# A graph layer on one core: two PSUM banks for the gathers, the marks in shared banks, narrower unread products, and a new order of all steps

## The chip, the cores and the metric

The kernel runs on one NeuronCore of a Trainium2 chip. The metric is the device time of one launch in microseconds (us). Three runs of the kernel before took 502.46, 503.40 and 503.78 us, the median is 503.40. One further execution was profiled and took 503.59 us.

The engines are named as in the profile: PE is TensorE (PEld is its loading of weights, which overlaps its products), DVE is VectorE, ACT is ScalarE, POOL is GpSimd, SP is SyncE, which issues the DMAs. L946 is line 946 of the kernel before.

## The reference, cut to what matters

128 graphs have 64 nodes each, a node has 128 channels, and about one in eight of the node pairs is an edge. Every edge sends a message through an MLP with two layer norms, messages are summed by receiving node, and a second MLP of the same form updates the node.

```python
def _mlp(x, w0, b0, g0, be0, w1, b1, g1, be1, w2, b2):
    h = relu(x @ w0 + b0)
    h = layernorm(h, g0, be0)
    h = relu(h @ w1 + b1)
    h = layernorm(h, g1, be1)
    return h @ w2 + b2

# x: (128, 64, 128), adj: (128, 64, 64) of 0 and 1
f_i, f_j = x[:, :, None, :], x[:, None, :, :]          # broadcast over the pairs
messages = _mlp(concat(f_i, f_j), *msg) * adj[..., None]
agg = sum(messages, axis=2)
return x + _mlp(concat(x, agg), *upd)
```

## The kernel before, in words

**Units of work.** Only edges are computed, not all 64 x 64 pairs. Each graph has 640 slots for its edges. Two graphs make a pair (64 pairs, index p), four pairs make a block (16 blocks, b), 512 slots make a chunk (160 chunks, n, ten to a block), and five chunks make a group (32 groups, q), for which the small statistics are worked out together.

**The edge path of one pair and its chunks.**
- `rank` (L744, DVE) and `count` (L753, PE) number the edges. `distance` (L889, ACT) and `make_tp` (L895, DVE) write for each slot the row i of its edge as a 0/1 table (tile tp).
- `marks` (L920, PE): for each half k of a pair's slots, one product of 128x320 in float16 gives the position of every slot within its row. Its result lies in PSUM in a tile mk. `compare` (L928, DVE) reads it and writes the 0/1 table for j. A bank of marks is free when the compare is done.
- `node_rows` (L904, POOL) and `stack` (L911, SP) put both tables below each other into one tile S of the pair by DMA (s<-i and s<-j). `node_marks` (L1034, SP) turns a table with a DMA transpose (oh).
- `rows` (L847, PE) computes x @ w0 for the nodes of half a block, split afterwards into a high and a low part (abh, abl; `rows_hi` L866 and L869, `rows_lo` L876, L877, L880).
- `gather` (L946, PE): product of abl and abh with S, which is the first layer of the edges of a chunk, in the bank hps. `relu0` (L951, ACT) reads it and writes h.
- `turn_h` (L956, PE) turns h into hT for `stats0` (L613, DVE). `seed` (L989 POOL, L993 ACT) prepares the bias, scaled by the standard deviation of the first norm.
- `layer1` (L1003, PE) is the second layer, in the banks z0 and z1; `relu1` (L597 DVE or L1012 ACT) writes y, `stats1` (L613, DVE) its statistics.
- `weights` (L1045, POOL) scales the receiving table by the second norm, and `reduce` (L1060, PE) sums the messages of a block into the bank ys.

**The node update of a block.** `turn` (L1109, PE) and `turn_out` (L1114, ACT) turn an operand of the update MLP (first ysum, then uh, then uy); `layer` (L1123, PE) applies a layer; `finish` (L1173, DVE) writes the result uo, and a DMA stores it. `turn_x` (L832, PE) turns the nodes' x.

**PSUM.** There are eight banks, one tile each, given out by pools (L663 to L669): `ps_k` for mk, `ps_h` for hps, `ps_t` for hT, two `ps_z`, `ps_y` for ys, `ps_a` (tile ma, by `abank`) and `ps_u` (tile mu, by `ubank`). ma takes the update turns, count, turn_x and the first half of the rows; mu takes the update layers and the second half of the rows. A step that asks for a bank waits until the last reader of the tile before it is done.

**The order.** Each step is entered with `at(n, place, fn)`: a slot n, about one per chunk, and a named place within the slot. A table `MOVE` (L24 to L357, 921 entries) shifts single steps to another slot, place or rank. The steps are then run in this order, and each one appends its instructions to the queues of the engines that it uses. So the order on PE, DVE, ACT, POOL and SP is fixed in the program, and an engine waits at the head of its queue until the semaphores of that instruction have come.

On PE, a block in the steady part runs in this order (T turn_h, L layer1, G gather, M mark): reduce, rows, rows, M, G, T, L, G, turn of ysum, T, L, G, L, T, M, G, update layer of xn and ysum, T, turn of uy, L, G, T, L, M, G, update layer, T, count, M, G, L, L, T, turn of uh, M, G, L, T, M, G, update layer, L, M, T, turn_x, L, G, T, M.

**Unread products.** `keep_busy` (L1322) puts products on PE that nobody reads, into the bank ys. A call with k over 4 makes k products of 128 columns, any other makes k // 2 products of 256 columns. Calls with numbers 7, 2, 4, 2, 4, 4 and 2 are entered before the first slot, and some more in the first slots; MOVE puts some of them much later.

Of the kernel before, what the change touches and what calls it, by code (L numbers as in the profile page):

```python
# [9 lines left out]
F32 = mybir.dt.float32  # L10
# [6 lines left out]
PSUM = bass.MemoryType.PSUM  # L17
# [7 lines left out]
    "<lambda>@@1": (1, "s", 1), "<lambda>@@10": (-1, "m", -1), "<lambda>@@11": (0, "T", 2),  # L25
    "<lambda>@@2": (1, "x", 2), "<lambda>@@3": (1, "S1", -1), "<lambda>@@4": (1, "k", 2),
    "<lambda>@@5": (0, "k", 2), "<lambda>@@6": (-1, "S1", -1), "<lambda>@@7": (-1, "T", 2),
    "<lambda>@@8": (0, "k", -5), "<lambda>@@9": (152, "L0", 3), "ahead@@0": (2, "x", 7),
    "ahead@@1": (2, "x1", -1), "ahead@@2": (1, "x1", 0), "ahead@@3": (2, "L1", -1),
    "ahead@@4": (1, "k", 3), "ahead@@6": (0, "T", 2), "bias0.@3": (-7, "a", 2),  # L30
    "bias0.@@143": (-1, "e0", 4), "bias0.@@153": (-9, "a", 2), "bias0.@@158": (-6, "e", -1),
    "bias0._0@@163": (-1, "T", 2), "bias0._2@@164": (-4, "L0", -1), "bounds@@152": (-136, "b", -1),
    "compare.0@0": (0, "e0", 0), "compare.0@2": (2, "k", 0), "compare.0@5": (1, "T", 0),
    "compare.0@7": (0, "m", 0), "compare.0@@0": (2, "x", 6), "compare.0@@10": (2, "e0", 3),
    "compare.0@@12": (2, "s", 1), "compare.0@@140": (-2, "S1", -1),
    "compare.0@@142": (-2, "k", -1), "compare.0@@145": (-3, "T", 0),
    "compare.0@@147": (-2, "x2", 2), "compare.0@@150": (2, "s", -1),
    "compare.0@@152": (2, "m", -2), "compare.0@@2": (2, "b", 2), "compare.0@@5": (1, "S1", 1),
    "compare.0@@7": (1, "L0", 0), "compare.1@1": (2, "T", -3), "compare.1@3": (3, "y", 2),
    "compare.1@6": (0, "x2", 2), "compare.1@8": (1, "s", 1), "compare.1@@1": (2, "x", 5),  # L40
    "compare.1@@11": (2, "T", -3), "compare.1@@13": (3, "a", 4), "compare.1@@138": (-1, "S1", 1),
    "compare.1@@141": (-2, "T", -1), "compare.1@@143": (-1, "b", 1),
    "compare.1@@146": (-1, "x", 2), "compare.1@@148": (3, "x", 2), "compare.1@@151": (2, "e0", 3),
    "compare.1@@153": (3, "b", 4), "compare.1@@3": (2, "x1", -2), "compare.1@@6": (2, "a", -1),
    "compare.1@@8": (2, "S1", 2), "compare_here@@-1#26": (3, "s", 1),
    "compare_here@@-1#31": (3, "s", 1), "compare_here@@-1#41": (3, "k", 4),
    "compare_here@@-1#47": (3, "x", -1), "count@8": (-2, "e0", -3), "count@@-1#6": (0, "e", -9),
    "count@@1": (1, "k", 5), "count@@138": (-2, "S1", -6), "count@@8": (1, "s", -3),
    "count_out@9": (-3, "e0", -1), "count_out@@-1#7": (0, "e", -9),
    "count_out@@139": (-3, "x", -4), "count_out@@2": (0, "x", 0), "count_out@@9": (0, "e1", 3),  # L50
    "degrees@9": (-6, "T", -2), "degrees@@-1#11": (1, "a", -1), "degrees@@139": (-3, "s", -2),
    "degrees@@2": (0, "s", 2), "degrees@@9": (0, "x1", 0), "distance@0": (-4, "k", -3),
    "distance@3": (1, "k", -1), "distance@5": (-3, "x", -2), "distance@8": (-2, "b", 1),
    "distance@@-1#13": (1, "x2", 0), "distance@@-1#27": (1, "e1", 1),
    "distance@@-1#33": (3, "y", 2), "distance@@1": (1, "k", 4), "distance@@10": (-3, "a", 1),
    "distance@@13": (2, "e", 2), "distance@@138": (-2, "a", -1), "distance@@140": (-3, "s", -1),
    "distance@@143": (-5, "S1", -2), "distance@@145": (-2, "y", 3), "distance@@148": (-7, "k", -1),
    "distance@@150": (-1, "x", 2), "distance@@3": (2, "k", 5), "distance@@5": (1, "y", -3),
    "distance@@8": (0, "x1", -1), "finish.@8": (2, "s", -2), "finish.@@138": (0, "x", -2),
    "finish.@@148": (6, "a", -1), "finish.@@158": (3, "S1", -1), "finish.@@168": (-1, "L0", -2),  # L60
    "finish.@@174": (32, "x1", 0), "finish._0@@175": (41, "e", -2), "finish._2@@176": (43, "y", 1),
    "flag_in@@153": (0, "T", -2), "flag_max@@156": (1, "x2", -1), "flag_out@@160": (2, "S1", -1),
    "flag_sum@@158": (4, "T", 0), "flag_turn@@155": (1, "k", 2), "gather@0": (-1, "m", -2),
    "gather@1": (-1, "b", 0), "gather@2": (1, "e", -1), "gather@3": (2, "L0", 4),
    "gather@4": (2, "m", 4), "gather@5": (1, "y", 1), "gather@6": (0, "T", 0),
    "gather@7": (-1, "k", -4), "gather@8": (-2, "x2", -2), "gather@9": (-2, "m", -2),
    "gather@@-1#28": (3, "y", 3), "gather@@-1#35": (3, "x1", -4), "gather@@-1#43": (4, "x", 1),
    "gather@@0": (3, "e0", 4), "gather@@1": (4, "L1", -5), "gather@@10": (1, "x2", -3),
    "gather@@11": (1, "e0", 3), "gather@@12": (2, "L1", -1), "gather@@13": (2, "e", 2),
    "gather@@138": (-2, "x2", -1), "gather@@139": (-3, "e1", -6), "gather@@140": (-3, "x2", 0),  # L70
    "gather@@141": (-3, "x2", -2), "gather@@142": (-2, "s", -1), "gather@@143": (-2, "s", 2),
    "gather@@144": (-2, "L0", -3), "gather@@145": (-3, "T", 0), "gather@@146": (-3, "S1", -2),
    "gather@@147": (-3, "a", 1), "gather@@148": (0, "x2", 0), "gather@@149": (0, "e1", -2),
    "gather@@150": (2, "s", -1), "gather@@151": (2, "m", 4), "gather@@152": (1, "x2", -2),
    "gather@@153": (0, "e1", -2), "gather@@154": (0, "e1", -2), "gather@@155": (1, "s", 1),
    "gather@@156": (0, "T", 0), "gather@@157": (0, "y", -1), "gather@@158": (0, "k", -1),
    "gather@@159": (0, "e", 2), "gather@@5": (0, "x1", -1), "gather@@6": (0, "y", -2),
    "gather@@7": (0, "a", 0), "gather@@8": (0, "k", -6), "gather@@9": (-1, "x1", -1),
    "inverse_of@0": (0, "x1", -1), "inverse_of@5": (1, "k", -2), "inverse_of@@140": (-3, "x", 1),
    "inverse_of@@145": (3, "x2", 1), "inverse_of@@150": (0, "x", -4),  # L80
    "inverse_of@@155": (2, "a", -2), "inverse_of@@160": (1, "L0", 3),
    "inverse_of@@165": (0, "m", 0), "inverse_of@@168": (2, "x2", -1), "keep@@1": (1, "x1", 0),
    "keep@@10": (0, "L0", 1), "keep@@2": (2, "b", -1), "keep@@3": (2, "L1", -6),
    "keep@@4": (1, "L1", -1), "keep@@5": (0, "k", 3), "keep@@6": (-1, "x1", -1),
    "keep@@7": (1, "s", -2), "keep@@9": (-1, "x1", 3), "keep_busy@@-1#0": (21, "x1", 0),
    "keep_busy@@-1#18": (3, "s", 1), "keep_busy@@-1#23": (17, "x2", -2),
    "keep_busy@@-1#30": (1, "e1", 1), "keep_busy@@-1#37": (17, "T", 2),
    "keep_busy@@-1#45": (3, "s", 1), "keep_busy@@-1#9": (17, "k", -5),
    "keep_busy@@2": (-3, "e", -7), "keep_busy@@3": (-4, "e", -3), "keep_busy@@4": (-5, "e", -7),
    "keep_busy@@5": (-4, "m", -1), "layer1@0": (-3, "m", -1), "layer1@1": (-2, "s", 1),  # L90
    "layer1@2": (-2, "e", 0), "layer1@3": (0, "b", -1), "layer1@4": (2, "m", 3),
    "layer1@5": (1, "y", 0), "layer1@6": (0, "L0", -3), "layer1@7": (-1, "k", -4),
    "layer1@8": (-2, "S1", -7), "layer1@9": (-2, "m", -1), "layer1@@10": (-1, "L1", 1),
    "layer1@@11": (1, "k", 0), "layer1@@12": (1, "e0", 0), "layer1@@13": (1, "L0", 3),
    "layer1@@138": (-2, "S1", -3), "layer1@@139": (-3, "x2", 2), "layer1@@140": (-3, "s", -2),
    "layer1@@141": (-4, "e1", 0), "layer1@@142": (-2, "m", 0), "layer1@@143": (-3, "S1", 2),
    "layer1@@144": (-2, "T", -1), "layer1@@145": (-3, "T", 0), "layer1@@146": (-3, "x", 0),
    "layer1@@147": (-3, "a", 1), "layer1@@148": (0, "a", 0), "layer1@@149": (1, "b", -2),
    "layer1@@150": (-1, "e1", -1), "layer1@@151": (1, "k", 2), "layer1@@152": (1, "T", -3),
    "layer1@@153": (1, "x", -2), "layer1@@154": (1, "m", -1), "layer1@@155": (1, "y", 8),  # L100
    "layer1@@157": (0, "y", -4), "layer1@@158": (0, "a", -2), "layer1@@159": (0, "x2", 1),
    "layer1@@160": (0, "x2", -2), "layer1@@161": (0, "L0", 3), "layer1@@162": (0, "T", -5),
    "layer1@@164": (1, "m", 1), "layer1@@165": (0, "b", 2), "layer1@@166": (0, "e0", 1),
# [256 lines left out]
def tile_gnn(  # L360
# [40 lines left out]
    nc = tc.nc  # L401
# [1246 lines left out]
```

## Time and profile before

| what | value |
|---|---|
| median of three runs | 503.40 us |
| lowest, highest | 502.46, 503.78 us |
| profiled execution | 503.59 us |
| its span | 501.7 us |
| mean clock granted to PE | 0.998 of full |
| PE busy | 491.1 us |
| PEld busy | 467.9 us |
| DVE, ACT, POOL busy | 460.5, 397.9, 353.8 us |
| first product on PE | 1.91 us |
| first gather | 11.17 us |
| last reduction, first instruction | 485.30 us |

The span is the time from the first to the last recorded instruction; 1.9 us of the profiled execution lie outside it. An instruction takes longer from its start to its end than from its start to the start of the next one, since products overlap: a turn of four products has 0.60 us from start to end, but the next step begins 0.44 us after it. What a step costs PE is the second number. A product of two 4-byte operands is recorded as two matmul records.

A row of the waits reads: the engine with its tile and line, "<-" the engine whose end released it, then the total in us, how often, and the longest. A row of the timeline begins with the start and the duration in us.

### The profile page before, as it was taken

How to read it: one execution, taken by the hardware profiler on the slowest of the kernel's cores; microseconds unless marked ns; L12 is line 12 of the kernel's file. 1: busy time of each engine (PE TensorE's matmuls, PEld its weight loads, DVE VectorE, ACT ScalarE, POOL GpSimd, SP SyncE). 2: the span in 40 equal slices, each digit the busy share in tenths (PEclk: the TensorE clock that was granted, in tenths of full speed). 3: DMA queues.
4: the chain of work that ended last, by engine and by line, in shares of the span. 5: the costliest groups of instructions: out<-in, count | busy, mean ns of one | idle time of the engine just before them, and what ended most of it. 6: DMA issues, size and time to landing. Idle time of an engine off the chain costs nothing.

```text
span 501.7 us, 15934 instructions
## 1 busy us (share of the span) xinstructions
PE 491.1 (98%) x5969; PEld 467.9 (93%) x5969; DVE 460.5 (92%) x1225; ACT 397.9 (79%) x907; POOL 353.8 (71%) x563
## 2 busy tenths in 40 slices
PE   8899999999999999999999999999999999999995
PEld 5799999999999999999999999999999999999984
DVE  7899789899999999998999999899999989998885
ACT  6999978889787788978778797877879778867753
POOL 3267686877869687786968768696886679674941
PEclk9999999999999999999999999999999999999999
DMA  4668565566948576684857757475564647345201
GB/s 122 157 138 170 122 129 130 114 133 137 164 104 153 126 141 131 130 161 107 160 128 113 157 121 162 104 171 123 121 154 111 156 107 171 88 113 107 63 23 46
DMA packets 91474, 63.55 MB, mean 127 GB/s; under 512 B 57473, under 2 KB 75522, under 8 KB 91394
## 3 DMA queue, kind: packets, MB, share of 16 engines
q1 hardware_dynamic: 91106, 62.36, 58.7%
q8 instruction: 49, 0.80, 0.7%
q14 instruction: 31, 0.25, 0.2%
q10 hardware_dynamic: 288, 0.13, 0.1%
HBM read 7.15 MB, written 4.19 MB: 23 GB/s over the span
## 4 chain that ended last, share of the span: by engine, by line


## 5 line engine op out<-in xcount | busy, mean ns | idle before, releaser
L1003 PE MATMUL z<-w1c,h 128*128 128x128 f32 x1280 | 167.4, 275 | 0.0
L1003 PEld LDWEIGHTS z<-w1c,h 128*128 128x128 f32 x1280 | 158.1, 192 | 4.1
L613 DVE BATCH_NORM_STATS2 st<-hT 128x6 f32<-128x256 f32 x320 | 120.3, 417 | 21.9 <-PE hT L956 18.7
L951 ACT ACTIVATE h<-hps,b0c 128x512 f32<-128x512 f32 x160 | 109.5, 684 | 24.3 <-PE hps L946 23.0
L993 ACT ACTIVATE z<-b1b,m_sd 128x128 f32<-128x128 f32 x320 | 118.8, 371 | 11.6 <-DVE y L597 4.6
L613 DVE BATCH_NORM_STATS2 st<-y 128x6 f32<-128x256 f32 x320 | 117.9, 417 | 0.1
L989 POOL TENSOR_TENSOR u<-b1b,m_sd 128x512 f32<-128x512 f32 x80 | 82.7, 1042 | 29.8 <-ACT m_sd L621 20.2
L956 PE MATMUL hT<-ident,h 128*128 128x128 f32 x640 | 96.6, 273 | 0.7 <-ACT h L951 0.7
L946 PE MATMUL hps<-s,abl 128*128 128x512 f32 (+3 forms) x256 | 93.4, 370 | 1.0 <-DMA s<-j 0.7
L1045 POOL TENSOR_TENSOR w<-oh,m_q 128x192 f32<-128x192 f16 x126 | 62.5, 509 | 39.9 <-issue 27.1
L956 PEld LDWEIGHTS hT<-ident,h 128*128 128x128 f32 x640 | 74.3, 141 | 1.9 <-ACT h L951 1.0
L946 PE MATMUL hps<-s,abh 128*128 128x512 f32 (+3 forms) x256 | 74.4, 322 | 0.0
L1012 ACT ACTIVATE y<-z 128x512 f32<-128x512 f32 x80 | 47.3, 594 | 30.9 <-PE z L1003 30.8
L928 DVE TENSOR_TENSOR j<-mk,cmpt 128x320 fp32r<-128x320 f32 x124 | 58.3, 470 | 1.4 <-PE mk L920 1.2
L597 DVE CUSTOM_DVE_ANT_0 y<-z,u 128x512 f32<-128x512 f32 x80 | 53.9, 674 | 3.9 <-PE z L1003 2.4
L889 ACT ACTIVATE d<-slot,mid 128x640 f16<-128x640 f16 x64 | 52.7, 826 | 0.7 <-DVE mid L799 0.7
L946 PEld LDWEIGHTS hps<-s,abl 128*128 128x128 f32 x256 | 48.7, 190 | 2.9 <-DMA s<-j 0.9
L946 PEld LDWEIGHTS hps<-s,abh 128*128 128x128 f32 x256 | 48.5, 189 | 0.0
L1060 PE MATMUL ys<-y,w 128*32 128x128 f32 x1488 | 44.3, 274 | 0.0
L1060 PEld LDWEIGHTS ys<-y,w 128*32 128x32 f32 x1488 | 39.7, 110 | 3.6 <-POOL w L1045 2.6
L904 POOL CAST i<-tp 128x640 fp32r<-128x640 f16 x58 | 42.4, 745 | 0.0
L920 PE MATMUL mk<-tp,posall 128*128 128x320 f16 x126 | 38.0, 302 | 0.2 <-DVE j L928 0.2
(195 smaller groups left out, 852.2 us busy)
## 6 DMA issues: line engine op xcount, KB each, us to landing
s<-i SPq DMA_DIRECT2D x124, 160.0 KB, 3.0
s<-j SPq DMA_DIRECT2D x124, 160.0 KB, 2.7
xn<-in_x_dram SPq DMA_DIRECT2D x15, 256.0 KB, 3.8
out_dram<-uo SPq DMA_DIRECT2D x15, 256.0 KB, 2.5
an<-in_adj_dram SPq DMA_DIRECT2D x16, 128.0 KB, 2.8
oh<-tp SPq DMA_TRANSPOSE x64, 3.2
xn<-in_x_dram SPq DMA_DIRECT2D x2, 128.0 KB, 2.8
out_dram<-uo SPq DMA_DIRECT2D x2, 128.0 KB, 3.6
```

The lines of the kernel that those rows point to most:

```text
L597: nc.vector._custom_dve(TENSOR_ADD_SAT, out=o, in0=ps, in1=sb, s0=BIG, s1=0.0)
L613: nc.vector.bn_stats(st, src.rearrange("p t c -> p c t"))
L889: nc.scalar.activation(D[p], slot, AF.Abs, bias=blocks[b]["mid"][:, q:q + 1], scale=-1.0)
L928: nc.vector.tensor_tensor(JR[p][:, c], MK.pop((p, k))[:, 0:HC], cmpt[:, c], op=ALU.is_equal)
L946: nc.tensor.matmul(ps[:, c:c + w], lhsT=ab[:, g % 4, :], rhs=s, start=(k == 0), stop=(k == 1))
L951: nc.scalar.activation(H[n], HP.pop(n), AF.Relu, bias=b0c)
L956: nc.tensor.transpose(ps[:, t, :], H[n][:, t * P:(t + 1) * P], ident)
L989: nc.gpsimd.tensor_tensor(U[n], bc(W["b1b"], CH), SR[q][:, k:k + CH].unsqueeze(2).to_broadcast([P, CH, C]), op=ALU.mult)
L993: nc.scalar.activation(z_of(n)[:, t, :], W["b1b"], AF.Copy, scale=SR[q][:, k + t:k + t + 1])
L1003: nc.tensor.matmul(ps[:, t, :], lhsT=h[:, t * P:(t + 1) * P], rhs=W["w1c"], start=added and t == 0, stop=True, skip_group_check=True)
L1045: (nc.vector if p == NP - 2 else nc.gpsimd).tensor_tensor(WT[p][:, g], oh, qs, op=ALU.mult)
L1060: nc.tensor.matmul(YS[b][g * N + m * HN:g * N + (m + 1) * HN, k, :], lhsT=w[:, g, m, u, :], rhs=y, start=(u == 0), stop=(u == TH - 1), til ...
```

## The change

Five things change in the program.
1. The bank of `ps_k` is given up, and `ps_h` has two buffers: the gathers take turns in two banks.
2. `marks` takes the bank ma for a pair's first half (k = 0) and the bank mu for its second (k = 1). Marks thus share ma with the update turns, count, turn_x and the first half of the rows, and mu with the update layers and the second half of the rows.
3. The first part of the last block's reduction, which was put into the bank of `ps_k`, goes into one of the gathers' banks.
4. `keep_busy` makes products of 128 columns only, k of them for k over 4 and k // 2 otherwise.
5. The table MOVE is written anew (923 entries in place of 921; of the 921 keys that both have, one has the same value). This gives a new order on PE, DVE, ACT, POOL and SP.

The number of instructions of each kind stays. On PE, a block of the steady part now runs in this order: reduce, rows, rows, T, turn of an update, L, M (ma), G, L, G, T, turn of an update, update layer, G, G, T, count, M (mu), L, L, T, M (ma), G, L, T, turn of an update, L, T, M (mu), G, M (ma), G, T, M (mu), L, update layer, turn_x, T, L, update layer, G, T, L, M (ma), G, M (mu), G, L, T.

```diff
-        ps_k = es.enter_context(tc.tile_pool(name="ps_k", bufs=1, space=PSUM))
-        ps_h = es.enter_context(tc.tile_pool(name="ps_h", bufs=1, space=PSUM))
+        ps_h = es.enter_context(tc.tile_pool(name="ps_h", bufs=2, space=PSUM))
...
-            MK[p, k] = bank() if bank else ps_k.tile([P, 512], F32, name="mk")
+            MK[p, k] = bank() if bank else ubank() if k else abank()
...
-                YS[b] = ps_k.tile([P, 512], F32, name="mk").rearrange("p (k c) -> p k c", k=PB)
+                YS[b] = hbank().rearrange("p (k c) -> p k c", k=PB)
...
-            if k > 4:
-                for _ in range(k):
-                    nc.tensor.matmul(warm[:, 0, :], lhsT=mean_m, rhs=mean_m, start=True, stop=True)
-            else:
-                for _ in range(k // 2):
-                    nc.tensor.matmul(warm[:, 0:2, :], lhsT=mean_m,
-                                     rhs=first.rearrange("p q j -> p (q j)"), start=True,
-                                     stop=True)
+            for _ in range(k if k > 4 else k // 2):
+                nc.tensor.matmul(warm[:, 0, :], lhsT=mean_m, rhs=mean_m, start=True, stop=True)
```

Of the new table, its `keep_busy` entries as an example of the form (key with its slot: shift in slots, place, rank):

```diff
-    "keep_busy@@-1#0": (21, "x1", 0), "keep_busy@@-1#18": (3, "s", 1), "keep_busy@@-1#23": (17, "x2", -2),
-    "keep_busy@@-1#30": (1, "e1", 1), "keep_busy@@-1#37": (17, "T", 2), "keep_busy@@-1#45": (3, "s", 1), "keep_busy@@-1#9": (17, "k", -5),
-    "keep_busy@@2": (-3, "e", -7), "keep_busy@@3": (-4, "e", -3), "keep_busy@@4": (-5, "e", -7), "keep_busy@@5": (-4, "m", -1),
+    "keep_busy@@-1#0": (13, "S1", 0), "keep_busy@@-1#18": (17, "e0", -1), "keep_busy@@-1#23": (1, "s", -11),
+    "keep_busy@@-1#30": (0, "e", -37), "keep_busy@@-1#37": (17, "b", 1), "keep_busy@@-1#45": (0, "e", -40), "keep_busy@@-1#9": (16, "e", 2),
+    "keep_busy@@2": (-3, "e", -4), "keep_busy@@3": (-4, "e", -5), "keep_busy@@4": (-3, "m", 2), "keep_busy@@5": (-6, "e", -1),
```

## The prediction

> **What bounds the kernel now.** I read the page's busy times first, then the same times by stretches of the span, then the waits of PE, then the timeline of PE.
>
> ```profile
> span 501.7 us, 15934 instructions
> PE 491.1 (98%) x5969; PEld 467.9 (93%) x5969; DVE 460.5 (92%) x1225; ACT 397.9 (79%) x907; POOL 353.8 (71%) x563
> ```
> ```profile
> 0.00:25.00 25.00, 21.46 (x189) 16.47 (x189) 19.98 (x57) 19.18 (x40) 7.09 (x21) 1.00 0.57 139
> 200.00:400.00 200.00, 200.00 (x2533) 193.71 (x2532) 190.67 (x504) 162.94 (x369) 152.12 (x238) 1.00 0.64 136
> 482.00:502.00 20.00, 13.16 (x138) 11.41 (x136) 11.78 (x36) 8.94 (x27) 4.60 (x9) 0.95 0.15 43
> ```
> The columns of the second fence are stretch, length, PE, PEld, DVE, ACT, POOL, clock, DMA share, GB/s. In the middle PE has work at every moment and DVE 95% of the time (190.67 of 200). Only the head and the tail show a PE that waits. The chain of waits is empty on this page, so I checked this with PE's own waits, which are small:
>
> ```profile
> PE ys L1329 <- DVE first L505: 1.9, 1, 1.9
> PE hps L946 <- DMA s<-j: 0.7, 1, 0.7
> PE hT L956 <- ACT h L951: 0.7, 2, 0.5
> ```
> and with the timeline of one block, from one reduction to the next:
>
> ```profile
> 212.21 2.83 PE L1060 MATMUL ys<-y,w 128*32 128x128 f32 x96
> 225.28 0.60 PE L956 MATMUL hT<-ident,h 128*128 128x128 f32 x4
> 225.72 0.60 PE L1109 MATMUL ma<-ident,uy 128*128 128x128 f32 x4
> 226.15 1.06 PE L1003 MATMUL z<-w1c,h 128*128 128x128 f32 x8
> 226.97 0.37 PE L946 MATMUL hps<-s,abl 128*128 128x256 f32 x1
> 228.85 0.30 PE L920 MATMUL mk<-tp,posall 128*128 128x320 f16 x1
> 241.65 2.06 PE L1060 MATMUL ys<-y,w 128*32 128x128 f32 x68
> ```
> A block takes 241.65 - 212.21 = 29.44 us. Start to next start gives what each step costs PE: a turn 0.437 (225.28 to 225.72), a layer1 0.895, a gather 0.476 to 0.53 by its pieces, a mark 0.125, rows 0.93 a half, reduction 2.74. A block holds 10 turns of h, 4 other turns, 10 layer1, 10 gathers, 8 marks, 2 rows, one reduction, one count and update layers of 1.79, 0.895 and 0.895: 6.12 + 8.95 + 4.98 + 1.0 + 1.86 + 2.74 + 0.03 + 3.58 = 29.26. So at most 0.18 us of a block is loss. The whole loss is about 9 us before 25 us, 2.5 us (14 x 0.18) spread over the blocks, about 2.5 us in irregular pieces (25 to 60 us, near 83, and 413 to 455; the largest is 0.5 at 454, ahead of a gather that waits for S), 2.8 us from 482 to 495.6, and 6 us after the last matmul.
>
> **What the Trainium skill says.** "Perfetto Trace Analysis", Identifying the Most-Contended Engine: matmul busy time is a poor measure, weight-load busy time a better one. PEld at 93% over the span, 97% (193.71 of 200) in the middle, agrees that PE is the bound. "PSUM — Partial Sum Buffer", PSUM bank collisions raise a hardware error: two engines may not touch one bank at once, so banks are guarded whole. A mark in a shared bank therefore waits for the whole copy out of it. Before shows such ordering only for other pairs of steps. "TensorE: Matmul & The Clock Gate", Architectural detail: VectorE and ScalarE run their queues strictly in order, so a late compare holds all behind it; the trace fits, the wait on DVE being for PE, 18.7 us for hT. Same page, Part 1: the clock starts at half and rises after a busy window of about 3.4 us. The trace agrees in kind:
>
> ```profile
> 1.91 2.08 PE L1329 MATMUL ys<-first,mean_m 128*128 128x256 f32 x4 [1.91 <-DVE first L505]
> 4.29 2.91 PE L1329 MATMUL ys<-first,mean_m 128*128 128x256 f32 x6
> 9.61 1.56 PE L1329 MATMUL ys<-first,mean_m 128*128 128x256 f32 x6
> ```
> The same record takes 2.08 / 4 = 0.52 us early and 1.56 / 6 = 0.26 us from 9.61 on; two records make one product.
>
> **The change part by part.** All sums are against the profiled run's 503.59 us (span 501.7 and 1.9 outside it). It lies 0.2 above the median of 503.4.
>
> *Unread products.* Products that lie where PE has other work cost their whole length. Before has four of 256 columns (0.435 each, 48.7 to 54.1 us) and seven of 128 (0.224 each, 60.3 to 61.8): 1.74 + 1.57 = 3.31. The built order of after has seven and five of 128 there: 12 x 0.224 = 2.69. That is **-0.62**. The rest lie in the first 10 us, where PE waits anyway: about 2 us less work, nothing gained, but see the second rival.
>
> *Two gather banks.* A gather's bank is free 1.0 us after its last matmul (relu0). Before puts 0.6 us or more of PE work between gathers, and no wait of a gather for relu0 is on the list of waits. At most 0.05 a block is to be had; I take **0**. The cover is the work between gathers; without it a gather would pay 0.4.
>
> *Marks in the banks of turns and update layers.* No instruction is added. In the order of after the closest neighbours in bank ma are an update turn and a mark with 0.895 of PE work between, 1.33 from the turn's start. In the trace the copy (ACT) ends 1.22 to 1.33 after the turn's start, and about 0.05 passes until PE goes on: 0 to 0.05 a block. In mu, a mark and the next layer start 1.02 apart; the compare ends 0.83 after its mark's start if DVE is free, but 1.94 in the median, because it queues on DVE. The same holds for two turns of h 1.70 apart, whose stats need 1.40 plus 0.05. I walked DVE through one block of after by hand (stats pair 0.68, relu 0.60, compare 0.41, finish 1.1): it keeps up, with under 0.1 us to spare where T, M, G, M, G, T, M, L and an update layer follow each other. Behind a late compare stand stats and relus, and for these the next turn and layer1 on PE. The loss lies between 0 (all in time) and 0.5 us a block; below nothing, a block has at most its 0.18 to give. I take 0.05 x 14 = **+0.7**.
>
> *New order, middle.* Of the 2.5 us of irregular loss, some must return, as the same tables load and the same S tiles land. DMA cover, counted as PE work from a pair's second mark to the first gather that reads it, is at least 5.4 us before and 6.2 after in a steady block; s<-i and s<-j take 2.7 to 3.0 us to land and 1.2 to 1.5 to issue, so SP's queue stays off the path. POOL at 71% stays off it too. Bounds -2.5 and +1; I take **-0.8**.
>
> *Head.* The first gather comes after some 0.9 us less of products, but an oh transpose (1.3 us of SP) now goes ahead of s<-j of an early pair. S of pair 2 is issued by 18.2 in both; before waited for it at 21.6. After has 8.5 us of useful work before that gather where before has 9.8. Bounds -0.15 and +1.15; I take **+0.3**.
>
> *Tail.* The last two part reductions (1.4 each) come after the last layer1 instead of around it, but fewer steps stand between them and the turn of ysum, and one POOL step stands ahead of the last finishes: -0.3 +- 1; I take **-0.3**.
>
> Sum: -0.62 + 0 + 0.7 - 0.8 + 0.3 - 0.3 = -0.7, so 502.9 for a run like the profiled one and **502.7** as the median.
>
> **Rivals.** *The shared banks stall on DVE (slower).* The compares at the dense run of marks come late, PE's mark, turn or layer waits, and this repeats in each of 14 blocks. For it: DVE is busy 95%, and one stats pair (0.68) queued ahead of a compare is enough to free its bank 0.6 late. Against: 18.7 us in which DVE waited for hT is reserve. At 0.3 us a block in place of 0.05: 503.4 - 1.4 + 4.2 = 506.2. It decides from about 0.2 us a block (2.9 us, less 1.4).
>
> *The clock rises late (slower).* With products half as long (six in before, about 1.0 each while slow, in 1.9 to 8.3 us; in after 0.5 each) PE is busy some 60% of this stretch, where before it was busy almost wholly from 1.9. If a window then counts as not busy, 3.4 us more run at half speed, once or twice; a part of this stretch is waiting anyway. +1 to +4; at 2.5: 502.7 + 2.5 = 505.2.
>
> *The new order removes the irregular losses (faster).* PE runs at its floor from 25 to 482: -0.62 - 2.5, and a tail shorter by 0.6: 503.4 - 3.7 = 499.7. For it: each loss is one late transfer or table. Against: the head's is bound by the loads.
>
> *Nothing but the products counts.* The banks and the order give what they take: 503.4 - 0.6 = 502.8, not apart from the forecast.
>
> **How the numbers follow.** Forecast (with the last rival) 0.36, stalls on DVE 0.32, late clock 0.12, floor 0.20. About 0.3% (1.5 us) is what a measurement of this kernel can tell from no change: faster is below 501.9, slower above 504.9. The forecast's own range is 501.2 to 504.3, and a quarter of it is faster: 0.10, with 0.19 of the floor case 0.29. Slower: 0.30 of the stalls, 0.08 of the clock, 0.02 of the forecast: 0.40. The rest, 0.31, is the same. The range 499.6 to 507.6 leaves out the lower end of the floor case and stalls beyond 0.4 us a block.
>
> **What would show it.** Right: blocks from reduction to reduction at 29.4 to 29.5, no wait of PE over 0.1 us for a compare or a copy, twelve late products of 0.224. Stalls: blocks at 29.7 or more, waits of PE for j or for copies from ma. Clock: records of 128 columns (0.224 / 2 = 0.112 apart at full clock) still at about twice that after 9 us. Wrong altogether: a gather that waits for S in every block, or a last matmul later against the last layer1.

## The result and the profile after

The changed kernel took 506.69 us in the median of four runs (505.94 to 508.57), the kernel before 503.27 beside it. The ratio is 1.0077, with a 95% interval of 1.006 to 1.0094: 3 to 4.7 us slower. The execution that was profiled took 508.57 us (span 506.8), the slowest of the four. So I had the same kernel profiled once more (507.22 us, span 505.4, median of 12 runs 506.77, ratio 1.0066, interval 1.0049 to 1.0083) and trust only what both traces show.

The page of the changed kernel:

```profile
span 506.8 us, 15927 instructions
PE 491.1 (97%) x5969; PEld 465.7 (92%) x5969; DVE 478.2 (94%) x1225; ACT 399.8 (79%) x907; POOL 354.9 (70%) x563
```

DVE is busy 17.7 us longer than before (460.5), with the same 1225 instructions. The stretches of the same trace (columns as in the prediction; in the second of them the kernel before had PE busy for all 200.00):

```profile
25.00:60.00 35.00, 33.45 (x370) 31.08 (x368) 33.71 (x82) 30.91 (x74) 22.93 (x35) 1.00 0.54 122
200.00:400.00 200.00, 199.95 (x2506) 192.73 (x2509) 198.69 (x504) 162.26 (x364) 152.00 (x237) 1.00 0.62 137
```

PE loses 1.5 us between 25 and 60 us, where before it lost nothing that shows. DVE is at 99% in the middle. Two waits of PE after 20 us that are larger than any of the kernel before there:

```profile
PE hT L958 <- DVE st L616: 1.5, 1, 1.5
PE hps L948 <- DVE u2c L543: 1.1, 1, 1.1
```

Neither is a mark that waits for a copy out of a shared bank, or an update turn or layer that waits for a compare. The second line names DVE, but its u2c was done long before; the gather waited for S (the pair's table, which the gathers read), and the second trace says so (1.7 us, for s<-i).

To see where the time went I took from each trace the start of every step on PE and subtracted the durations of all useful steps before it (471.24 us in both kernels). What is left is the loss: time in which PE waited, ran slowly or ran unread products. The loss in us, by stretches:

| useful work done by PE (us) | before | changed, second trace | changed, with three moves (see below) |
|---|---|---|---|
| 0 to 20 (until about 34 us) | 13.25 | 14.20 | 12.91 |
| 20 to 60 (about 34 to 80 us) | 4.19 | 5.79 | 4.51 |
| 60 to 400 | 3.06 | 4.09 | 2.90 |
| 400 to 460 | 1.42 | 0.98 | 0.97 |
| 460 to the last layer | 2.66 | 3.33 | 3.53 |
| sum | 24.58 | 28.39 | 24.82 |

28.39 - 24.58 = 3.8 us: 1.0 in the head, 1.6 in the first full block, 1.0 spread over the blocks, 0.7 at the end, and 0.4 regained ahead of it. Four places, four questions. (The stretch from 20 to 60 holds all late unread products, 3.31 us before and 2.69 after. Without them its loss grew by 2.2.)

### The profile page after: what moved, and what is told of

Read it like the earlier page. It is cut to its first block, busy times and chain, and to the rows that moved or that the text cites. A ratio compares the mean times of both kernels' runs of the same rounds, so it can differ in the third digit from the quotient of the medians.

```text
span 506.8 us, 15927 instructions
## 1 busy us (share of the span) xinstructions
PE 491.1 (97%) x5969; PEld 465.7 (92%) x5969; DVE 478.2 (94%) x1225; ACT 399.8 (79%) x907; POOL 354.9 (70%) x563
## 3 DMA queue, kind: packets, MB, share of 16 engines
HBM read 7.15 MB, written 4.19 MB: 22 GB/s over the span
## 5 line engine op out<-in xcount | busy, mean ns | idle before, releaser
L953 ACT ACTIVATE h<-hps,b0c 128x512 f32<-128x512 f32 x160 | 107.0, 681 | 12.4 <-PE hps L948 11.7
L958 PEld LDWEIGHTS hT<-ident,h 128*128 128x128 f32 x640 | 72.8, 141 | 9.7 <-PE ma L922 3.1
L600 DVE CUSTOM_DVE_ANT_0 y<-z,u 128x512 f32<-128x512 f32 x80 | 54.2, 677 | 3.0 <-POOL w L1047 1.6
L634 POOL TENSOR_TENSOR m_v<-m_v,st 128x20 f32<-128x20 f32 x31 | 7.2, 232 | 52.4 <-DVE st L616 50.5
L897 DVE TENSOR_SCALAR tp<-d,deg 128x640 f16<-128x640 f16 x64 | 43.2, 679 | 0.3 <-ACT d L891 0.3
L906 POOL CAST i<-tp 128x640 fp32r<-128x640 f16 x58 | 40.9, 717 | 0.8 <-DMA s<-i 0.5
```

What stands on the lines that cost most here:

```text
L600: nc.vector._custom_dve(TENSOR_ADD_SAT, out=o, in0=ps, in1=sb, s0=BIG, s1=0.0)
L953: nc.scalar.activation(H[n], HP.pop(n), AF.Relu, bias=b0c)
L958: nc.tensor.transpose(ps[:, t, :], H[n][:, t * P:(t + 1) * P], ident)
```

## The experiments

My first theory was the rival of the prediction in part: DVE is late. Against it stood the clock (the records of the head reach full speed at 12.3 us in the second trace, at 8.7 before), the banks, and a path that I had set aside, the queue of SP.

### The same kernel again

> The changed kernel once more, nothing edited. Its profiled execution (508.57 us) was the slowest of four, 1.9 above their median. If the losses of that trace are properties of the order (the 1.5 us stall of a turn of h near 54 us, the slow DVE steps beside POOL), they are there again: DVE busy 478 +- 2 us, the stall near 54 us within 0.3. If the difference lies in when the clock rises, full speed comes at another moment than 13.7 us and the execution is nearer 506.5. Median 506.7 +- 0.5 in both cases.

DVE was busy 477.8 us, and the turn of h at 54 us waited for DVE again (1.55 us on the timeline below). Records came to full speed at 12.3 us instead of 13.7. So the stall belongs to the order, and the four places stand.

### Is it the clock and the width of the products?

The first edit, in the changed kernel:

```diff
-            for _ in range(k if k > 4 else k // 2):
-                nc.tensor.matmul(warm[:, 0, :], lhsT=mean_m, rhs=mean_m, start=True, stop=True)
+            for _ in range(k if k > 4 else k // 2):
+                if k <= 4 and len(early_busy) < 8:
+                    early_busy.append(k)
+                    nc.tensor.matmul(warm[:, 0:2, :], lhsT=mean_m,
+                                     rhs=first.rearrange("p q j -> p (q j)"), start=True,
+                                     stop=True)
+                else:
+                    nc.tensor.matmul(warm[:, 0, :], lhsT=mean_m, rhs=mean_m, start=True, stop=True)
```

> The changed kernel, but the eight unread products of the first 11 us are 256 columns wide again (the late ones stay at 128). If the clock rose late because PE had too little work, the records are at full speed before 10 us again and the time falls by 1 to 3 us, to about 505. If the head is set by the loads and by DVE, the time stays within 0.5 us of the changed kernel, or rises by up to 0.5, since wider products delay what follows them.

Measured: 507.15 us, ratio to before 1.0071 (1.0044 to 1.0098). Full speed did come some 4 us sooner (at 8.1 us, in place of 12.3), and the median did not fall; the interval leaves room for about 1 us. (The profiled execution, 505.72 us, was the second shortest of six.) The second edit gives the kernel before the `keep_busy` of the changed one:

```diff
-            if k > 4:
...
-            else:
-                for _ in range(k // 2):
-                    nc.tensor.matmul(warm[:, 0:2, :], lhsT=mean_m,
...
+            for _ in range(k if k > 4 else k // 2):
+                nc.tensor.matmul(warm[:, 0, :], lhsT=mean_m, rhs=mean_m, start=True, stop=True)
```

> The kernel before, with its unread products of 256 columns cut to 128. If narrow products let the clock rise late, the head loses 1 to 3 us and the four late products give back 4 x (0.435 - 0.224) = 0.84: about 504.5 to 505.5. If the clock doesn't depend on them, only the 0.84 is left: 502.5.

Measured: 502.81, ratio 0.9992 (0.9978 to 1.0007). Narrow products cost the kernel before nothing, nor is a gain of 0.84 sure. But they did not make its clock late either (full speed at 8.1 us, with wide products at 8.7), so this run doesn't say what a late clock costs. The traces of the changed kernel do. Its head came to full speed at 11.0 us in a later run that has the same head (the second run under "The end once more"), at 12.3 in the second trace and at 13.7 in the first. The first gather of pair 2 began at the same time in all three, here in this order:

```profile
22.57 0.42 PE L1537 MATMUL hps<-s,abl 128*128 128x384 f32 x1 [2.13 <-DMA s<-i]
22.59 0.41 PE L948 MATMUL hps<-s,abl 128*128 128x384 f32 x1 [1.72 <-DMA s<-i]
22.44 0.41 PE L948 MATMUL hps<-s,abl 128*128 128x384 f32 x1 [1.13 <-DVE u2c L543]
```

The later the clock, the shorter the wait for S: the late clock only used time in which PE would have waited. So it doesn't by itself cost the head its 1.0 us. The kernel before reaches its gather of this pair at that moment too:

```profile
22.57 0.50 PE L946 MATMUL hps<-s,abl 128*128 128x512 f32 x1 [0.69 <-DMA s<-j]
```

It has done about 1.2 us more of useful work by then. That is the head's loss. One thing stays open: with wide early products this gather began at 21.68 and the head lost 0.9 us less, though the copies were issued no sooner (s<-j at 16.05 us, against 15.96 in the second trace).

### What does the end cost?

The kernel before, with the 155 table entries of slots 158 and up that differ taken from the changed kernel, as these:

```diff
-    "gather@@158": (0, "k", -1), "gather@@159": (0, "e", 2),
+    "gather@@158": (3, "s", 0), "gather@@159": (3, "L0", 2),
...
-    "finish._2@@176": (43, "y", 1),
+    "finish._2@@176": (72, "a", 2),
```

> The kernel before, with the entries of the order table for slots 158 and up (the last update blocks, the last reductions, the finishes) taken from the changed kernel. If the new tail costs 1.3 us by itself, as the two traces say (3.4 us of PE loss after 482 us against 2.1), the time is 504.5. If the loss in the tail came from what went before it, the time stays at 503.3. My forecast of the tail was -0.3, which would give 503.0.

Measured: 506.14, ratio 1.006 (1.0043 to 1.0078), more than the 1.3 us. The trace says why it is more than the end:

```profile
467.41 0.50 PE L1537 MATMUL hps<-s,abl 128*128 128x512 f32 x1 [1.46 <-ACT h L1542]
```

(The table is written with one entry per line there, so line numbers are higher.) Here an order made for two gather banks runs on one, and a gather waits 1.46 us for relu0 to leave it. That is what the second bank is worth to this order, and it was worth nothing to the other. From useful work 460 on, the loss is 3.34, as in the changed kernel (3.33) and 0.7 above that of before. In both, PE waits at the end for copies by ACT for which the kernel before doesn't wait. In the second trace of the changed kernel they are:

```profile
486.62 0.49 PE L1125 MATMUL mu<-w2u,ysumT 128*128 128x128 f32 x2 [0.45 <-ACT ysumT L1116]
489.18 0.49 PE L1125 MATMUL z<-w2u,ysumT 128*128 128x128 f32 x2 [0.29 <-ACT ysumT L1116]
496.35 0.71 PE L1125 MATMUL z<-u1c,uhT 128*128 128x128 f32 x4 [0.54 <-ACT uhT L1116]
```

A layer follows the turn of its own operand there with at most 0.22 us of other work between, and waits for the copy. The kernel before loses 0.38 there at another place, to a wait for DVE (uo).

### DVE beside POOL

Where did DVE's 17.7 us come from? From two operations, by form; the kernel before first:

```profile
L895 DVE TENSOR_SCALAR tp<-d,deg 128x640 f16<-128x640 f16 x64 | 29.3, 457 | 0.0
L824 DVE SCALAR_TENSOR_TENSOR a<-an 128x256 f32<-128x256 f32 x16 | 13.0, 812 | 0.0
```

and the changed one:

```profile
L897 DVE TENSOR_SCALAR tp<-d,deg 128x640 f16<-128x640 f16 x64 | 43.2, 679 | 0.3 <-ACT d L891 0.3
L826 DVE SCALAR_TENSOR_TENSOR a<-an 128x256 f32<-128x256 f32 x16 | 19.1, 1194 | 0.0
```

14 and 6 us more for the same instructions (busy us and mean ns stand after the bar). The timeline ahead of the stall, in the second trace of the changed kernel:

```profile
46.66 1.04 POOL L1100 TENSOR_TENSOR m<-c2u,deg 128x512 f32<-128x512 f32 x1
46.69 1.56 DVE L746 TENSOR_TENSOR_SCAN rk<-first,an 128x256 f16<-128x256 f32 x1
...
47.78 1.54 POOL L1101 TENSOR_TENSOR m<-m,ub0r 128x512 f32<-128x512 f32 x1
48.17 1.33 DVE L897 TENSOR_SCALAR tp<-d,deg 128x640 f16<-128x640 f16 x1
...
50.05 1.28 POOL L879 TENSOR_TENSOR abl<-ab,abh 128x512 fp32r<-128x512 f32 x1
50.10 1.41 DVE L897 TENSOR_SCALAR tp<-d,deg 128x640 f16<-128x640 f16 x1
...
54.35 0.63 PE L958 MATMUL hT<-ident,h 128*128 128x128 f32 x4 [1.55 <-DVE st L616]
```

Each slow DVE step begins just after a POOL step has begun, and ends soon after that ends (make_tp at 50.10 ends 0.18 after POOL's L879, the scan 0.55 after L1100). Undisturbed, the scan takes 0.68 and make_tp 0.36. The Trainium skill, "SBUF — State Buffer", Who interferes with whom, gives a reason that fits: DVE and GpSimd share a pair of SBUF ports, as an exclusive lock for a whole instruction. A tensor_scalar in a fast mode needs it, and so does an operation with two SBUF inputs where GpSimd's reads SBUF too, and whichever issues first holds the other up. The trace agrees: 0.36 against 1.41. In the trace with wide early products the two steps begin within 0.01 us of each other; there the scan kept its 0.68, and it was POOL's step that took 1.52 in place of 1.04.

Three runs test it. The first moves only bias0 of the first block (POOL's L1100 and L1101 above):

```diff
                 n, pr = n + dn, (pr if n + dn < 0 else 0) + dp
+            if fn.__name__ == "bias0" and args[0].b == 0:
+                n += 4
```

> The changed kernel; the two POOL steps of bias0 (1.04 and 1.28 us) of the first block alone are put four slots later, everything else as it was. In two traces of the changed kernel they run from 46.5 to 49.2 us, beside a scan of 1.58 and a make_tp of 1.34 on DVE that take 0.68 and 0.37 elsewhere, and a turn of h waits 1.7 us for DVE at 54 us. If POOL's steps make these DVE steps slow and this makes the stall, the two are 0.7 and 0.4 again, the stall is below 0.3 and the time falls by 1 to 1.7 us, to 505.0 to 505.7. If DVE is late for another reason, the stall stays and the time is 506.7.

Measured: 505.83, ratio 1.0051 (1.0032 to 1.007), 0.9 below the changed kernel. The timeline:

```profile
46.16 0.68 DVE L748 TENSOR_TENSOR_SCAN rk<-first,an 128x256 f16<-128x256 f32 x1
46.75 0.36 DVE L899 TENSOR_SCALAR tp<-d,deg 128x640 f16<-128x640 f16 x1
...
47.67 1.28 POOL L881 TENSOR_TENSOR abl<-ab,abh 128x512 fp32r<-128x512 f32 x1
48.03 1.09 DVE L899 TENSOR_SCALAR tp<-d,deg 128x640 f16<-128x640 f16 x1
```

Scan and first make_tp are at 0.68 and 0.36, the third step still meets POOL's L881, and the stall of a turn near 54 us is gone from the waits. The ratios alone don't tell 0.9 us from nothing (the intervals overlap); the vanished wait does, and with it the loss of the stretch from 20 to 60 us of useful work, which is about 1.8 less than in the second trace.

The second takes bias0 and residual of all blocks to the places of before, 13 entries of the table:

```diff
-    "bias0.@3": (-8, "m", 3), "bias0.@@143": (-2, "T", -3), "bias0.@@153": (-18, "S1", -3),
+    "bias0.@3": (-7, "a", 2), "bias0.@@143": (-1, "e0", 4), "bias0.@@153": (-9, "a", 2),
...
-    "residual.@9": (-4, "m", 2), "residual.@@139": (-4, "e", 3),
+    "residual.@9": (-3, "x2", -3), "residual.@@139": (3, "x", -2),
...
```

> The changed kernel with the table entries of bias0 and residual (three long POOL steps of a block) taken from the kernel before; all other entries are those of the changed kernel. If what slows DVE's steps (make_tp 0.68 in the mean against 0.46, the step of odd_weights 1.19 against 0.81) is these POOL steps beside them, DVE's busy time falls from 478 towards 465 and the time by 1 to 3 us. If other POOL steps then stand beside them, DVE stays at 475 to 480 and the time within 0.7 of 506.7.

Measured: 510.87, ratio 1.0154 (1.0115 to 1.0193), 4 us slower than the changed kernel, while DVE's busy time fell to 459.6, that of before. Among its waits of PE is a new one:

```profile
PE hps L1537 <- DMA s<-j: 3.6, 4, 2.8
```

So DVE's slowness comes from these POOL steps, as expected. The time says less: by the trace the stall near 54 us is gone here too, but after 380 us about 5 us are lost anew, 2.8 of them where a gather waits for S; why S came late there isn't shown. In the blocks between, nothing was gained from DVE's 18 us. The control leaves out `odd_weights`, DVE's search for adjacency values other than 0 and 1, in both kernels:

```diff
-            an = blocks[b]["an"]
-            a2 = adp.tile([P, PB, N], F32, name="a2")
-            nc.vector.scalar_tensor_tensor(a2, an, 1.0, an, op0=ALU.subtract, op1=ALU.mult)
-            nc.vector.tensor_reduce(nball[:, b:b + 1], a2.rearrange("p q j -> p (q j)"),
-                                    axis=AX.X, op=ALU.max, apply_absolute_value=True)
+            return
```

> The changed kernel without odd_weights, the two DVE steps of a block that look for adjacency values other than 0 and 1 (their result is set to zero once); that part of the computation is left out. It takes 1.19 + 0.42 = 1.6 us of DVE from every block. If DVE's lateness is what the changed kernel pays for, its time falls by 2 to 3.5 us, to about 504, and the kernel before falls by less than 0.8 with the same edit. If PE's own order, the loads or the banks are at fault, it falls by no more than the kernel before does.

> The kernel before without odd_weights, as a control of the same edit; the search for adjacency values other than 0 and 1 is left out. 0.81 + 0.42 = 1.2 us of DVE less in every block. PE is at its floor in the middle, so 0 to 0.8 us less: 502.4 to 503.2. If DVE bounds this kernel as well, 2 us or more.

Measured: 507.26, ratio 1.0069 (1.0041 to 1.0096), and 503.78, ratio 1.0011 (0.9998 to 1.0025). DVE was busy 12 us less in the changed kernel (465.9; the steps left out had taken 26, but make_tp took 54.2 in place of 43.2) and the time did not fall; the stall at 54 us stood at 1.5 us. My theory as stated, that the changed kernel pays for a full DVE, is refuted. DVE at 99% in the middle still delivers in time. What costs is one place, in the first full block, where DVE has no lead and three of its steps in a row are held up by 0.9 to 1.05 us each.

### The queue of SP

Two places remain in which gathers wait for S. The copies into S and the transposes oh are issued by SP, one after the other. The head of the changed kernel, second trace (start and length of the issue):

```profile
14.52 1.33 SPq L1036 DMA_TRANSPOSE oh<-tp  x1
15.96 1.18 SPq L913 DMA_DIRECT2D s<-j  x2
```

The prediction saw this transpose and took +0.3 for it. The edit moves it alone:

```diff
                 n, pr = n + dn, (pr if n + dn < 0 else 0) + dp
+            if fn.__name__ == "node_marks" and args[0] == 0:
+                n += 2
```

> The changed kernel with one DMA step moved: the transpose of the first pair's table (oh, 1.33 us of SP's queue at 14.5 us) is issued two slots later, behind the copies into S of pair 2. If those copies come late because the transpose is queued ahead of them, the wait of a gather near 22 us (1.7 us in one trace of the changed kernel, 1.1 in the other) falls below 0.7, as in the kernel before, and the time by about 1.0, to 505.8. If the copies are late because the transfers themselves are slow, or the step before them is, the wait and the time stay (506.7).

```profile
15.10 1.19 SPq L915 DMA_DIRECT2D s<-j  x2
...
17.61 1.36 SPq L1038 DMA_TRANSPOSE oh<-tp  x1
```

Measured: 505.56, ratio 1.0051 (1.0037 to 1.0064), about 1.1 less by the medians; the interval overlaps that of the second measurement of the changed kernel. The copies go out 0.85 us sooner, and the gather begins at 21.64, 0.95 us sooner, after a wait of 0.9 us in place of 1.7: expected in size, though not below 0.7.

In a steady block, the changed kernel puts three transposes ahead of 6 us of copies (first trace):

```profile
183.31 2.55 SPq L1036 DMA_TRANSPOSE oh<-tp  x2
...
186.58 1.21 SPq L1036 DMA_TRANSPOSE oh<-tp  x1
187.88 2.37 SPq L913 DMA_DIRECT2D s<-i  x2
190.30 2.53 SPq L913 DMA_DIRECT2D s<-j  x4
192.94 1.18 SPq L913 DMA_DIRECT2D s<-i  x2
```

The kernel before has at most one between copies (two once, near 412 us):

```profile
181.71 1.10 SPq L911 DMA_DIRECT2D s<-j  x2
182.91 1.27 SPq L1034 DMA_TRANSPOSE oh<-tp  x1
184.83 2.40 SPq L911 DMA_DIRECT2D s<-i  x4
```

The gather that needs the last of these copies starts at 196.75, 2.6 us after the last issue ended, and PE loses 0.6 us in it. This block lasts 30.28 us from reduction to reduction (30.15 in the second trace; a count below 96 means that the view ended within the reduction):

```profile
188.62 2.61 PE L1062 MATMUL ys<-y,w 128*32 128x128 f32 x88
218.90 2.83 PE L1062 MATMUL ys<-y,w 128*32 128x128 f32 x96
```

The edit, for all pairs but the first, leaves one transpose there:

```diff
+            if fn.__name__ == "node_marks" and args[0]:
+                n += 1
```

> The changed kernel with all other transposes oh one slot later: in a steady block, one of them instead of three is then queued on SP between a copy s<-j and the next four copies into S. If this queue is what makes gathers wait for S in some blocks (0.3 to 0.8 us near 107, 137, 197 and 284 us, in other blocks in other executions), these waits go and the time falls by about 1 us, to 505.7. If the waits come from the transfers being many at once, they stay: 506.7 +- 0.4. If the weights get late instead, it is slower.

Measured: 506.34, ratio 1.0056 (1.0032 to 1.008). The same block lasts 29.44, and every one from 128 to 364 us is at 29.4 to 29.6:

```profile
187.51 2.72 PE L1064 MATMUL ys<-y,w 128*32 128x128 f32 x92
216.95 2.83 PE L1064 MATMUL ys<-y,w 128*32 128x128 f32 x96
```

Over useful work from 60 to 350 us the loss is 2.43, against 3.55 in the second trace of the changed kernel and 2.24 before. The trace confirms 1.1 us; the median shows only 0.4 to 0.5, which the interval doesn't tell from nothing. The two later runs that have this move, too, keep these blocks at 29.4 to 29.6; every other trace of the changed order has one or more from 29.7 us up.

All three moves at once:

```diff
+            if fn.__name__ == "bias0" and args[0].b == 0:
+                n += 4
+            if fn.__name__ == "node_marks":
+                n += 2 if args[0] == 0 else 1
```

> The changed kernel with three moves at once: bias0 of the first block four slots later, the first transpose oh two slots later, all other transposes one slot later. If the stall on DVE at 54 us, the late S of pair 2 and the queue of transposes are separate causes, their parts add up: 0.9 + 1.0 + 1.0 less, 503.8. If one stall only covers the next (what is removed from one wait is waited for later), the sum is clearly less than the parts: 505 or more.

Measured: 504.74 in the median of 20 runs, ratio 1.0039 (1.0023 to 1.0055). That is 2.0 less than the changed kernel (1.4 to 1.9 by the ratios), of the 2.9 that were expected; the trace (503.35 us, near the fastest of the 20) has 24.82 of loss, as before has. What stays above before in it is the end (3.53 against 2.66).

### The late unread products

The prediction took them at their whole length. The kernel before without them:

```diff
         def keep_busy(k):
 
+            if len(busy) >= 9 or k > 4:
+                return
+            busy.extend(range(k // 2))
             if k > 4:
```

> The kernel before without the four wide and seven narrow unread products between 48 and 62 us; its nine early products stay. If PE is at its floor there, as I took it in the prediction, they cost their whole length: 3.3 us less, 499.7. If they filled time in which PE would wait for another engine anyway, the time stays above 502.

Measured: 501.96, ratio 0.9975 (0.9961 to 0.9988): 0.6 to 2.0 us less, not 3.3. Between 46 and 64 us PE now waits:

```profile
PE hT L956 <- DVE st L613: 0.8, 2, 0.5
PE mk L920 <- DVE j L928: 0.3, 1, 0.3
```

The products stood where PE would have waited for DVE. Counted as busy time they made PE look bound by its own work. This kernel beats both others, so I added the move of bias0:

```diff
+            if fn.__name__ == "bias0" and args[0].b == 0:
+                n += 4
```

> The kernel before without its eleven late unread products, and with bias0 of the first block four slots later. Without these products PE waited for DVE between 48 and 63 us (2.2 us in all), and DVE there runs behind a make_tp of 1.18 us at 38.5 us beside the first POOL step of bias0. If DVE's slow step is carried on to these waits, 0.5 to 0.8 us are gained over the 1.0 of the run without products: 501.3. If DVE's queue is full there anyway, it stays at 502.0, or gets slower if bias0 meets other DVE steps at its new place.

Measured: 501.68, ratio 0.9971 (0.9958 to 0.9985). The same as without the move, to within the interval. The turns near 49 and 51 us wait 0.5 and 0.3 us for DVE without the move, 0.35 and 0.3 with it. This says little on a full queue, as the slow make_tp did not go: it took 0.85 us at 38.3 us in place of 1.18.

### The end once more

Two runs take only the 53 entries of slots 170 and up that differ from before, with the three moves and without:

```diff
-    "residual._2@@170": (59, "s", 2), "turn._0.uh@@171": (5, "x1", 2),
+    "residual._2@@170": (5, "y", -2), "turn._0.uh@@171": (6, "L0", 0),
...
-    "finish._2@@176": (72, "a", 2),
+    "finish._2@@176": (43, "y", 1),
```

> The changed kernel with the three moves of the run before (bias0 of the first block four slots later, the first transpose two slots, the others one slot) and, beside them, the entries of the order table for slots 170 and up, which order the last update blocks and the end, taken from the kernel before. The traces put 0.7 to 0.8 us of the remaining difference after 482 us. If that is a matter of these last entries, the time is about 504.0; if of the order of the last reductions, which stays, 504.7.

> The changed kernel with only the entries of the order table for slots 170 and up taken from the kernel before. If the end alone is worth 0.7, 506.0; if it isn't these entries, 506.7. The difference to the run above tells once more what the three moves are worth together: 2.0 by the first measurement.

Measured: 505.76, ratio 1.0063 (1.0039 to 1.0086), and 508.04, ratio 1.01 (1.0066 to 1.0134). Both are slower by about 1 us than without these entries, since a turn now waits for DVE in the end:

```profile
489.81 0.66 PE L1700 MATMUL ma<-ident,uh 128*128 128x128 f32 x4 [0.91 <-DVE uh L1189]
```

(second run). So the 0.7 us of the end could not be undone by its last entries: two of the three waits for ACT shown above are gone, and this one has come instead. What in the order brings them about stays open. The difference of the two runs, 2.3 us, is the worth of the three moves a second time, after 2.0.

## Why the prediction was wrong

Forecast 502.7, measured 506.7, a change of +3.4 where -0.7 was expected. By its steps:

- *Unread products, -0.62.* Failed. "Products that lie where PE has other work cost their whole length" was read from a PE that was busy at every moment. It was busy partly with these products. 3.31 us of them, taken out, gave about 1.3 us by the ratio. What shortening them gave to the changed kernel was not measured by itself.
- *Two gather banks, 0.* Right, in that no gather gained by it; one bank under the new order costs 1.46 us at one gather. The price of "0.4" without cover was too low.
- *Marks in shared banks, +0.7.* The trace shows no wait for these banks in the steady blocks, so the lower part of the bounds, 0 to 0.05 a block. The banks alone, under either order, were not tried: a step would ask for a bank whose last reader stands behind it in the order.
- *DVE by hand.* Failed in its durations: the walk used 0.68, 0.60 and 0.41 and no make_tp or scan that POOL holds up. With make_tp at 1.3 and 1.4 and a scan at 1.56 in a row, the 0.1 us to spare was gone in one block, and a turn waited 1.5 to 1.6 us. It did keep up in the others, also at 99%.
- *New order, middle, -0.8.* Failed, with the wrong sign: +1.6 near 54 us (2.2 with the unread products taken apart), +1.0 in the blocks, -0.4 ahead of the end. The sentence that failed is "SP's queue stays off the path. POOL at 71% stays off it too". I had counted DMA cover from a pair's second mark, which is the way of j. The copies stand behind transposes on SP, three at 1.2 to 1.3 us each; moving these took 1.1 us of loss from the blocks. And a share of time busy says nothing about such a queue, nor about POOL, whose steps hold up DVE.
- *Head, +0.3.* The mechanism was right (a transpose ahead of s<-j, and 8.5 us of useful work ahead of the gather in place of 9.8), the size was not: S comes at the same time as before, so nearly all of these 1.3 us turns into waiting. +1.0, inside the bounds.
- *Tail, -0.3.* +0.7 by the traces, at the edge of its bounds. It left out that a layer would wait for the copy of its own turn (0.45, 0.29 and 0.54 us).
- *Rivals.* The slower one, "The shared banks stall on DVE", gave 506.2, close to the truth, for a reason that the runs don't support: not the banks, not every block, and DVE held up by POOL instead of by its own queue. The late clock was real (12.3 and 13.7 us in place of 8.7), but the head waited for S whatever the clock did.

The three moves leave 504.74 against 502.94, 1.8 us. The two traces differ by only 0.2 us of loss (0.87 more at the end, 0.63 less elsewhere), as the profiled execution of the moved kernel was among the shortest of its 20. So most of the 1.8 lies in executions that were not profiled, and its place stays open.

## What to carry to other kernels

A filler that nobody reads counts as busy: before calling an engine bound by its own work, subtract its fillers and look for who would be late there. When an order is changed, walk every in-order queue past each moved step, the DMA-issuing one first, and price steps of DVE by what POOL runs beside them, not by their mean. A busy share of 99% or 71% decides nothing by itself; the place with no lead does.

## What the runs showed of the hardware beside this

- The same pair of instructions can hold each other up either way: scan 1.56 beside POOL 1.04 where POOL's step began 0.03 us ahead, or scan 0.68 beside POOL 1.52 where they began within 0.01 us.
- From the last 32-column product of `rows` to the next step PE takes 0.20 us in both kernels, where neighbouring products of full width lie 0.11 apart; from the last full product to the first of the reduction the changed kernel takes 0.20 too. So a change of width costs about 0.09 us each way.
- With eight early unread products half as wide, the changed kernel came to full clock at 12.3 and 13.7 us in its two traces, with wide ones at 8.1. The kernel before came to it at 8.1 us with narrow products and at 8.7 with wide ones. So the width alone doesn't decide it, and what does isn't shown.
